# Three parts of an attention schedule moved: layer norm statistics six steps sooner, expert weights four steps later, the last output tile in the fourth step

## The chip, the cores and the metric

The kernel runs on one core of a Trainium2 chip. A core has a matrix engine (TensorE, written PE; PEld is its loading of weights), a vector engine (VectorE, DVE), an engine for activations (ScalarE, ACT), a general engine (GpSimd, POOL), and SyncE (SP), which here only issues transfers (DMAs). Each engine works through its own queue of instructions in order and waits on semaphores for the others. Matrix products land in PSUM banks; ACT or DVE must copy them out (evict them) before the bank is used again. The metric is the device time of one execution in microseconds, the median of several.

## The reference

For each of 16 batch elements of 512 tokens with 128 features, in float32:

```python
mod = (silu(c) @ wmod).reshape(16, 6, 1, 128)      # sa, ca, ga, sb, cb, gb
ga, gb = [(2*(g >= 0) - 1) * maximum(abs(g), 0.25) for g in (ga, gb)]
h = layernorm(x) * (1 + ca) + sa
x = x + ga * attention(h)            # 16 heads of 64, causal softmax, W_out, b_out
h = layernorm(x) * (1 + cb) + sb
logits = h @ Wr + br                 # 8 experts, the two largest are kept
weights = softmax(where(logits >= second_largest, logits, -inf))
expert_out = gelu(h @ W1 + b1) @ W2 + b2           # each expert, hidden size 512
x = x + gb * sum_over_experts(expert_out * weights)
```

## The kernel before

The kernel has two phases. The first does attention, both layer norms and the routing of tokens to experts; the second runs the experts over tiles of 256 routed rows and adds the results up. The change is in the first.

**Elements, pairs, steps.** The loop over `pairs` (near the end of the main function) goes over the 16 elements b and, in each, over 8 pairs of heads n = 0 to 7. One turn is a step; step n of element b is called step n below, counted from 0. `attend` writes out a step in a fixed order on PE, DVE, ACT and SP, because `manual_schedule` keeps the written order of these four engines; GpSimd's instructions are chained to their order by `Pinned`. In a step, PE does the scores of this pair (L446), z of the previous pair (L534), the q and k projection of the next pair (L410), then what `units` holds, then the transposes of the probabilities (L506). DVE takes the masked maxima (L463) and the reciprocals (L486), then what `c` holds, then copies two of the three transposed groups out of PSUM (L516). ACT takes the exponentials (L479), evicts z (L543) and q and k (L418), and copies the third transposed group (L516). POOL multiplies the probabilities by the reciprocals (L116, the helper line of all its pinned calls).

**PSUM.** The pool `ring` has four buffers of two banks, given out in turn. A product that takes a buffer waits until what stood in it four allocations earlier has been evicted.

**Work beside.** `BESIDE` says for each step which tasks of other elements go into it. `quiet` is behind this step's maxima on GpSimd, `a` and `b` stand between reciprocals on DVE, `units` on PE, `c` before the pT copies on DVE, `last` at the end. A letter names the element: `s` the next one (its first layer norm, transposition and v projection), `f` the previous one (output projection, second layer norm, router logits), `r` the one before that (routing), `m` this one. `BESIDE_LAST` holds the same for the last element. `1` is one indirect store of routed rows on GpSimd, two of them in steps 0 and 1.

The tasks that matter here:

- `ln0`, `ln1` (`layernorm`, L326 to L329): bn_stats and bn_aggr for two token tiles each, on DVE, and after the second an addition of epsilon. `dev` raises this to the power -0.5 on POOL; `norm0`, `norm1` (L338) normalise on DVE; `hT` transposes on PE and is evicted by ACT (L696). They serve the first norm (`s`) or the second (`f`).
- `o0`, `o1` (`project_out`): the output projection of token tiles 0 and 1, and 2 and 3: for each tile 8 head pairs with two column halves, 64 matmul instructions in the profile. `add0`, `add1` (`projected`, L615) add the bias on DVE; `x0`, `x1` (`attended`) multiply by the gate and add to x on POOL.
- `share`, `choose`, `count`, `rank`, `extend`, `place`, `pick`, `carry`: routing, small operations on DVE and one product on PE. `extend` starts at L828 with `lack`, `place` ends at L861; `pick` ends with the weights of the chosen experts (L873, L874).
- `load_x` (L137): the load of an element's x, issued by SP at step 0 of the element before it.

**SP at the start.** After the weights, SP issues in element 0 `load_rest` and, at the end of step 1, `lay_out` (L258 to L277): copies of the experts' weights within device memory and fills of the buffers `hs` (10 MB) and `ys` (1 MB) with zeros. Behind these come the loads of `mods` (L227, at the end of step 7) and of x_2 (at step 0 of element 1); x_0 and x_1 are loaded before all of it.

Of the kernel before, what the change touches and what calls it, by code (L numbers as in the profile page):

```python
# [9 lines left out]
FP = mybir.dt.float32  # L10
# [5 lines left out]
P = 128  # L16
# [5 lines left out]
def kernel(  # L22
# [65 lines left out]
    def bank(name):  # L88
        return banks(name)[:, 0, :]
# [43 lines left out]
    x_tiles = {}  # L133

    def load_x(b):
        x = work.tile([P, NT, D], FP, tag="x", name=f"x_{b}", bufs=3)
        nc.sync.dma_start(out=x, in_=resid[b].rearrange("(t p) d -> p t d", p=P))  # L137
        x_tiles[b] = x

# [383 lines left out]
    def z(b, n, ps=None):  # L523
        v, pT = v_tiles[b, n // (NP // VH)], pT_tiles.pop((b, n))
        col = n % (NP // VH) * P
        if ps is None:
            ps = bank(f"ps_z_{b}_{n}")


        for t in reversed(range(NT)):  # L530
            for own in (True, False)[: NT - t]:
                cols = slice(t * P, (t + 1) * P) if own else slice((t + 1) * P, S)
                for j in range(2):
                    nc.tensor.matmul(  # L534
                        ps[j * DH : (j + 1) * DH, cols],
                        v[:, t, col + j * DH : col + (j + 1) * DH],
                        pT[:, t, j, cols],
                        start=(t == NT - 1),
                        stop=(t == 0 and not own),
                    )  # L540
        zT = work.tile([P, S], FP, tag="zT", name=f"zT_{b}_{n}", bufs=NP + 2)
        zT_tiles[b, n] = zT
        return lambda: nc.scalar.copy(zT, ps)  # L543

# [50 lines left out]
    hT2 = {}  # L595
    attn_out = {}

    def project_out(b, half_of):
        ps = bank(f"ps_o_{b}_{half_of}")
        attn_out[b, half_of] = ps  # L600
        for t in range(2 * half_of, 2 * half_of + 2):
            for n in range(NP):
                in_columns(
                    ps[:, ts(t % 2, D)],
                    zT_tiles[b, n][:, ts(t, P)],
                    wo_sb[:, n, :],
                    start=(n == 0),
                    stop=(n == NP - 1),
                )

    def projected(b, half_of):
        if half_of == 0:
            attn_sum[b] = work.tile([P, NT, D], FP, tag="o", name=f"o_{b}", bufs=1)
        ps = attn_out.pop((b, half_of))
        nc.vector.tensor_tensor(  # L615
            attn_sum[b][:, 2 * half_of : 2 * half_of + 2, :],
            ps[:, : 2 * D].rearrange("p (t d) -> p t d", d=D),
            bo_sb.unsqueeze(1).to_broadcast([P, 2, D]),
            ALU.add,
        )  # L620

# [101 lines left out]
    def finishing(b):  # L723

        return in_parts(
            b,
            mods=(load_mods,),
            o0=(project_out, 0),
            o1=(project_out, 1),
            add0=(projected, 0),  # L730
            add1=(projected, 1),
            x0=(attended, 0),
            x1=(attended, 1),
            ln0=(layernorm, 1, 0),
            ln1=(layernorm, 1, 1),
            dev=(deviation, 1),
            off=(offset,),
            norm=(second_norm,),
            store=(store,),
            hT=(second_hT,),  # L740
            lg=(logits,),
            wt=(weights,),
            share=(share,),
        )
# [30 lines left out]
    def route(b):  # L775
# [85 lines left out]
            nc.vector.tensor_tensor(pos, pos, room, ALU.add)  # L861

        def pick():
            wt, _ = chosen_by.pop(b)
            chosen = tiles["chosen"]
            part = tmp("part", both)
            pos = tiles["pos"]
            nc.vector.tensor_tensor(part, chosen, pos.unsqueeze(1).to_broadcast(both), ALU.mult)
            where = tmp("where", [P, 2, NT])
            nc.vector.tensor_reduce(where, part, AX.X, ALU.add)  # L870
            slots_of[b] = tmp("slot", [P, 2, NT], I32, bufs=2)
            nc.vector.tensor_copy(slots_of[b], where)
            nc.vector.tensor_tensor(part, chosen, wt.unsqueeze(1).to_broadcast(both), ALU.mult)  # L873
            nc.vector.tensor_reduce(weight[:, :, at], part, AX.X, ALU.add)  # L874

# [8 lines left out]
        def experts():  # L884
# [21 lines left out]
            nc.sync.dma_start(out=rows_of[first], in_=in_dram.rearrange("s o -> o s"))  # L906

        parts = dict(
            choose=choose, count=count, rank=rank, extend=extend, place=place, pick=pick, carry=carry_on
        )  # L910
        if b in (LATE - 1, LAST):
            parts["experts"] = experts
# [200 lines left out]
    x2 = {}  # L1113

    def fetch_x(b):
        x2[b] = work.tile([P, NT, D], FP, tag="zT", name=f"x2_{b}", bufs=NP + 2)
        nc.sync.dma_start(out=x2[b], in_=kept(x_rows[b]))
        load_gate_b(b)

    def combine(b, width=NT):  # L1120

        x, got = x2.pop(b), got_tiles.pop(b)
        gb = gates_b.pop(b)
        y = work.tile([P, NT, D], FP, tag="zT", name=f"y_{b}", bufs=NP + 2)
        results[b] = y
        for t in range(0, NT, width):
            part = slice(t, t + width)
            for u in range(t, t + width):
                i = b * NT + u
                nc.scalar.activation(y[:, u, :], got[:, 0, u, :], AF.Identity, scale=weight[:, 0, i : i + 1])  # L1130
            for u in range(t, t + width):
                i = b * NT + u
                nc.vector.scalar_tensor_tensor(
                    y[:, u, :], got[:, 1, u, :], weight[:, 1, i : i + 1], y[:, u, :], ALU.mult, ALU.add
                )
            nc.vector.tensor_tensor(
                y[:, part], y[:, part], gb.unsqueeze(1).to_broadcast([P, width, D]), ALU.mult
            )
            nc.vector.tensor_tensor(y[:, part], y[:, part], x[:, part], ALU.add)
            if width < NT:  # L1140
                stored.setdefault(b, []).append(
                    nc.sync.dma_start(out=in_rows(out[b])[:, part], in_=y[:, part]).ins
                )
# [79 lines left out]
    def dense_rest(b):  # L1223

        h = work.tile([P, NT, D], FP, tag="hT1", name=f"rest_h_{b}")
        nc.sync.dma_start(out=h, in_=kept(h2_rows[b]))
        x = work.tile([P, NT, D], FP, tag="x", name=f"rest_x_{b}", bufs=3)
        load = nc.sync.dma_start(out=x, in_=in_rows(out[b]))
        behind_all(load.ins, stored.get(b, ()), "the element's output so far")
        hT = work.tile([P, S], FP, tag="hT2", name=f"rest_hT_{b}", bufs=1)  # L1230
# [26 lines left out]
    for task in later:  # L1257
# [2 lines left out]


    BESIDE = {
        0: dict(a="r.share", b="r.choose", quiet="1", units="f.o0 r.count", c="1 s.ln0 f.add0 r.rank",
                last="f.x0"),
        1: dict(quiet="1", units="f.o1", c="1 s.ln1 r.extend r.place f.add1", last="s.dev f.x1"),
        2: dict(b="s.norm0", quiet="1", units="v0", c="s.norm1 r.pick", last="rows"),
        3: dict(units="s.hT", c="f.ln0"),
        4: dict(quiet="1", units="v1", c="f.ln1 r.carry", last="f.dev"),
        5: dict(a="f.off", quiet="1", units="s.v0", c="f.norm"),
        6: dict(quiet="1", units="s.v1 f.hT", last="f.store"),  # L1270
        7: dict(units="f.lg", c="f.wt", last="m.mods"),
    }

    BESIDE_LAST = {
        0: dict(a="r.share", b="r.choose", quiet="1", units="f.o0 r.count", c="1 f.add0 r.rank", last="f.x0"),
        1: dict(quiet="1", units="f.o1", c="1 r.extend r.place f.add1", last="f.x1"),
        2: dict(quiet="1", units="v0", c="r.pick", last="rows"),
        3: dict(quiet="1", units="v1", c="1 f.ln0 r.carry", last="r.experts"),
        4: dict(quiet="1", c="1 f.ln1", last="f.dev"),
        5: dict(a="f.off", quiet="1", c="1 f.norm"),  # L1280
        6: dict(quiet="1", units="f.hT", c="1", last="f.store"),
        7: dict(units="f.lg o01234", c="f.wt", late="o56", last="m.mods"),
    }

    FIRST = {
        0: dict(units=[begin["v0"], begin["v1"], modulation_matmuls], c=[modulation_rows], last=[load_rest]),
        1: dict(units=[transposed_b1], c=[copied_b1], last=[lay_out]),
    }
    ends = finishing(LAST)
    for at, (b, n) in enumerate(pairs):  # L1290
        prev = pairs[at - 1] if at else None
        nxt = pairs[at + 1] if at + 1 < len(pairs) else None
        if n == 0 and b + 1 < B and b + 1 not in x_tiles:
            load_x(b + 1)
        if n == 7 and b < LAST:
            routes[b - 1] = route(b - 1) if b else {}
        known = {
            "s": starting(b + 1) if b + 1 < B else {},
            "f": finishing(b - 1) if b else {},
            "r": routes.get(b - 2, {}) | ({"share": finishing(b - 2)["share"]} if b > 1 else {}),  # L1300
            "m": finishing(b),
# [57 lines left out]
        10: ["share"],  # L1359
    }  # L1360
    steps = {at: [ends[name] for name in names] for at, names in steps.items()}
    for at, name in enumerate(("share", "choose", "count", "rank", "extend", "place", "pick", "carry")):
        steps.setdefault(1 + at, []).append(routes[LATE][name])
    for k, part in enumerate([*routes[LAST].values(), left_here, left_all]):
        steps.setdefault(11 + k, []).append(part)
# [93 lines left out]
```

## Time and profile before

| what | value |
|---|---|
| median of 3 executions | 1553.93 us (1552.44 to 1553.98) |
| the profiled execution's own time | 1554.75 us |
| its span, first to last instruction | 1552.9 us |
| PE / DVE / ACT / POOL busy | 97% / 71% / 68% / 62% |
| granted TensorE clock, mean | 0.993 |
| one element of the first phase (element 8, eight steps) | 77.8 us |

The table and the numbers of the prediction come from one profiled execution. The page gives busy times over the whole span; the windows give them for a stretch (sum, mean, clock and the transfers' share at the end of a line); the timeline lists instructions with start, duration, engine, line, operation, output and inputs, and in square brackets how long the engine stood idle before it and what ended that wait. A step is measured here from the first scores matmul to the first scores matmul of the next step. Busy time of PE is modelled at its ends, so a full PE in a window says that it had work, not that it ran at its peak.

### The profile page before, as it was taken

The page shows a single profiled execution, that of the slowest core. Times are in us where ns is not written, and L with a number is a line of the kernel's source. Part 1 is how long each engine was busy: PE and PEld are TensorE (multiplying, and loading weights), DVE is VectorE, ACT ScalarE, POOL GpSimd, SP SyncE. Part 2 cuts the span into 40 slices and gives each one's busy share as a digit, 9 for nine tenths or more (in the row PEclk, how much of TensorE's full clock was granted, in tenths as well). Part 3 has the DMA queues.
Part 4 walks back from the last instruction along what each step waited for, and adds up shares of the span by engine and source line. Part 5 has one row for each costly group of instructions (what it writes and reads, how often), then busy time and mean ns, then how long its engine had stood idle before and what let it go on. Part 6 is the DMA issues. An engine that isn't in the chain of part 4 may idle for free. (4 is left out here: it accounts for less than half of the span.)

```text
span 1552.9 us, 45385 instructions
## 1 busy us (share of the span) xinstructions
PE 1506.9 (97%) x16760; PEld 1042.5 (67%) x16760; DVE 1098.2 (71%) x4264; ACT 1062.5 (68%) x2885; POOL 964.1 (62%) x1555
## 2 busy tenths in 40 slices
PE   6999999999999999999999999999999999999994
PEld 3565656565656565656666666666666679999994
DVE  4767787878787878787878787878787844443434
ACT  4767777777777777777777777777777754444543
POOL 3445556666666666666666666666666656667653
PEclk9999999999999999999999999999999999999997
DMA  3860101010101010101010101010100047799994
GB/s 112 216 185 9 36 12 36 22 36 22 36 22 36 22 36 22 36 22 36 22 36 22 36 23 36 22 36 22 36 22 29 28 139 246 239 348 317 308 305 141
DMA packets 97902, 130.79 MB, mean 84 GB/s; under 512 B 10777, under 2 KB 73166, under 8 KB 97674
## 3 DMA queue, kind: packets, MB, share of 16 engines
q1 hardware_dynamic: 86777, 102.17, 21.4%
q0 software_dynamic: 10608, 24.73, 4.6%
q8 instruction: 135, 2.21, 0.6%
q10 hardware_dynamic: 288, 0.92, 0.2%
q14 instruction: 94, 0.76, 0.2%
HBM read 86.95 MB, written 46.07 MB: 86 GB/s over the span
## 5 line engine op out<-in xcount | busy, mean ns | idle before, releaser
L479 ACT ACTIVATE p<-p,nmax 128x512 f32<-128x512 f32 (+3 forms) x1024 | 560.3, 549 | 216.6 <-DVE nmax L463 216.6
L116 POOL TENSOR_SCALAR p<-p,rden 128x512 f32<-128x512 f32 (+3 forms) x1024 | 527.9, 533 | 240.4 <-DVE rden L486 233.4
L463 DVE CUSTOM_DVE_ANT_0 p<-sc,mask 128x512 f32<-128x512 f32 (+3 forms) x1024 | 439.9, 485 | 12.8 <-PE sc L446 12.4
L516 DVE COPY pT<-ps_pT 128x1024 f32<-128x1024 f32 (+2 forms) x384 | 276.5, 771 | 82.5 <-PE ps_pT L506 81.9
L446 PE MATMUL sc<-qk 64*128 64x512 f32 (+3 forms) x2048 | 312.8, 443 | 4.2 <-DVE pT L516 1.5
L534 PE MATMUL ps_z<-pT,v 128*64 128x128 f32 x3556 | 303.5, 322 | 0.2
L116 POOL DMA_INDIRECT hs<-rows,slot x128 | 134.8, 1053 | 215.4 <-DVE nmax L463 143.7
L446 PEld LDWEIGHTS sc<-qk 64*128 64x128 f32 x2048 | 185.5, 189 | 117.6 <-DVE pT L516 57.5
L534 PEld LDWEIGHTS ps_z<-pT,v 128*64 128x64 f32 x3556 | 200.5, 137 | 33.8 <-PE sc L446 0.5
L506 PEld LDWEIGHTS ps_pT<-ident,p 64*128 64x128 f32 x5120 | 177.2, 139 | 64.2 <-POOL p L116 56.8
L506 PE MATMUL ps_pT<-ident,p 64*128 64x64 f32 x5120 | 201.6, 226 | 10.3 <-POOL p L116 6.9
L1019 ACT ACTIVATE hid<-ps_h,wexp 128x256 f32<-128x256 f32 x272 | 106.8, 476 | 128.0 <-issue 120.0
L479 ACT ACTIVATION_READ_ACCUMULATOR p<-p,nmax 128x1 f32 x1024 | 191.3, 187 | 0.0
L486 DVE RECIPROCAL rden<-den 128x2 f32<-128x2 f32 x512 | 84.0, 164 | 146.3 <-ACT p L479 141.8
L116 POOL DMA_INDIRECT ys<-yrow,to_rows x136 | 134.9, 992 | 63.6 <-issue 28.0
L516 ACT COPY pT<-ps_pT 128x768 f32<-128x768 f32 x128 | 102.1, 798 | 98.7 <-PE ps_pT L506 96.1
L410 PE MATMUL ps_qk<-hT,wq_sb 128*64 128x512 f32 x512 | 132.6, 596 | 0.9 <-ACT hT L696 0.9
L410 PE MATMUL ps_qk<-hT,wk_sb 128*64 128x512 f32 x512 | 132.5, 596 | 0.0
L1032 PE MATMUL ps_e<-wexp,hid 128*128 128x128 f32 x1088 | 132.4, 275 | 0.0
L418 ACT COPY qk<-ps_qk 128x1024 f32<-128x1024 f32 x128 | 128.6, 1005 | 3.8 <-PE ps_qk L410 3.8
L1017 PE MATMUL ps_h<-hsT,wexp 128*128 128x256 f32 x544 | 129.5, 381 | 1.3 <-DVE hsT L1005 1.3
L1032 PEld LDWEIGHTS ps_e<-wexp,hid 128*128 128x128 f32 x1088 | 126.8, 192 | 0.1
(140 smaller groups left out, 1490.2 us busy)
## 6 DMA issues: line engine op xcount, KB each, us to landing
wexp<-wall SPq DMA_DIRECT2D x68, 578.0 KB
hs<-empty SPq DMA_DIRECT2D x1, 10062.0 KB
hrow<-hs SPq DMA_DIRECT2D x68, 129.0 KB
rows<-h_rows SPq DMA_DIRECT2D x32, 256.0 KB
got<-ys POOLq DMA_DIRECT2D x15, 512.0 KB, 5.2
x<-in_L_attn_resid_dram SPq DMA_DIRECT2D x16, 256.0 KB
mods<-mods_rows SPq DMA_DIRECT2D x16, 256.0 KB
x_rows<-x SPq DMA_DIRECT2D x16, 256.0 KB
```

Source lines behind the costliest of these rows:

```text
L116: made = getattr(nc.gpsimd, name)(*args, **kw)
L410: nc.tensor.matmul(out[r], lhsT[:, r], rhs, **flags)
L418: evictions.append(lambda: nc.scalar.copy(qk, ps))
L446: nc.tensor.matmul(ps[:, j, off : off + w], qk[r, 0, ts(i, P)], qk[r, 1, :w], start=True, stop=True)
L463: masked = nc.vector.tensor_tensor_reduce(out=p[:, j, r], in0=ps[:, j, r], in1=mask[:, S - (i + 1) * P : S], scale=-QSCALE, scalar=-MASKED ...
L479: nc.scalar.activation(p[:, j, r], p[:, j, r], AF.Exp, bias=nmax[:, j : j + 1], scale=-1.0, accum_out=den[:, j : j + 1])
L506: nc.tensor.transpose(ps[:, h, off + 2 * t + j, :], p[rows, j, at + t * P : at + (t + 1) * P], ident[rows, rows],)
L516: engine_copy(pT[:, : 2 * (i + 1), ts(i, P)].rearrange("p k (h q) -> p k h q", h=2), ps[:, :, off : off + 2 * (i + 1), :].rearrange("p h k ...
L534: nc.tensor.matmul(ps[j * DH : (j + 1) * DH, cols], v[:, t, col + j * DH : col + (j + 1) * DH], pT[:, t, j, cols], start=(t == NT - 1), st ...
L1017: nc.tensor.matmul(parts[j], wts[:, ts(j, P)], hT, start=True, stop=True)
L1019: nc.scalar.activation(hid[:, j, :], parts[j], AF.Gelu, bias=wts[:, ROWW - NHC + j : ROWW - NHC + j + 1])
L1032: nc.tensor.matmul(ps[:, ts(c, D)], hid[:, j, ts(c, P)], wts[:, HID + j * D : HID + (j + 1) * D], start=(j == 0), stop=(j == NHC - 1),)
```

## The change

Three tasks move, and two pools grow to allow it.

- The first layer norm's `ln0`, `ln1` and `dev` leave steps 0 and 1, where they served the next element (`s`), for steps 5 and 6, where they serve the element after the next (`t`, two ahead). x is therefore loaded at step 4, two elements ahead, and the pool of x has 4 buffers. Element 1's statistics, which no earlier element can take, stand in `FIRST`, in steps 0 and 1 of element 0, where they were.
- The output projection is cut into three parts, token tiles 0 and 1, tile 2, and tile 3: `o1` and `add1` in step 1 are half as large, and `o2`, `add2` and `x1` stand in step 3. In step 1, `add1` stands ahead of `extend` and `place`; in step 3, `add2` ahead of `ln0`. The zT pool has one more buffer, since tile 3 of all eight pairs is read until step 3.
- The weights of the chosen experts become a task of their own, `weigh`, in step 6; `pick` keeps the slots in step 2.
- For the last element, `v1` moves from step 3 to step 4, and `o2` takes its place.

```diff
     def load_x(b):
-        x = work.tile([P, NT, D], FP, tag="x", name=f"x_{b}", bufs=3)
+        x = work.tile([P, NT, D], FP, tag="x", name=f"x_{b}", bufs=4)
...
-        zT = work.tile([P, S], FP, tag="zT", name=f"zT_{b}_{n}", bufs=NP + 2)
+        zT = work.tile([P, S], FP, tag="zT", name=f"zT_{b}_{n}", bufs=NP + 3)
...
+    OUT = ((0, 1), (2,), (3,))
+
+    def project_out(b, part):
+        ps = bank(f"ps_o_{b}_{part}")
+        attn_out[b, part] = ps
+        for k, t in enumerate(OUT[part]):
             for n in range(NP):
                 in_columns(
-                    ps[:, ts(t % 2, D)],
+                    ps[:, ts(k, D)],
...
-    def projected(b, half_of):
-        if half_of == 0:
+    def projected(b, part):
+        if part == 0:
             attn_sum[b] = work.tile([P, NT, D], FP, tag="o", name=f"o_{b}", bufs=1)
-        ps = attn_out.pop((b, half_of))
+        ps = attn_out.pop((b, part))
+        n = len(OUT[part])
         nc.vector.tensor_tensor(
-            attn_sum[b][:, 2 * half_of : 2 * half_of + 2, :],
-            ps[:, : 2 * D].rearrange("p (t d) -> p t d", d=D),
-            bo_sb.unsqueeze(1).to_broadcast([P, 2, D]),
+            attn_sum[b][:, OUT[part][0] : OUT[part][0] + n, :],
+            ps[:, : n * D].rearrange("p (t d) -> p t d", d=D),
+            bo_sb.unsqueeze(1).to_broadcast([P, n, D]),
             ALU.add,
         )
...
+        def weigh():
+            wt, _ = chosen_by.pop(b)
+            chosen = tiles["chosen"]
+            part = tmp("part", both)
             nc.vector.tensor_tensor(part, chosen, wt.unsqueeze(1).to_broadcast(both), ALU.mult)
             nc.vector.tensor_reduce(weight[:, :, at], part, AX.X, ALU.add)
...
     BESIDE = {
-        0: dict(a="r.share", b="r.choose", quiet="1", units="f.o0 r.count", c="1 s.ln0 f.add0 r.rank",
-                last="f.x0"),
-        1: dict(quiet="1", units="f.o1", c="1 s.ln1 r.extend r.place f.add1", last="s.dev f.x1"),
+        0: dict(a="r.share", b="r.choose", quiet="1", units="f.o0 r.count", c="1 f.add0 r.rank", last="f.x0"),
+        1: dict(quiet="1", units="f.o1", c="1 f.add1 r.extend r.place"),
         2: dict(b="s.norm0", quiet="1", units="v0", c="s.norm1 r.pick", last="rows"),
-        3: dict(units="s.hT", c="f.ln0"),
+        3: dict(units="s.hT f.o2", c="f.add2 f.ln0", last="f.x1"),
         4: dict(quiet="1", units="v1", c="f.ln1 r.carry", last="f.dev"),
-        5: dict(a="f.off", quiet="1", units="s.v0", c="f.norm"),
-        6: dict(quiet="1", units="s.v1 f.hT", last="f.store"),
+        5: dict(a="f.off", quiet="1", units="s.v0", c="f.norm t.ln0"),
+        6: dict(quiet="1", units="s.v1 f.hT", c="r.weigh t.ln1", last="f.store t.dev"),
         7: dict(units="f.lg", c="f.wt", last="m.mods"),
     }
 
     BESIDE_LAST = {
-        0: dict(a="r.share", b="r.choose", quiet="1", units="f.o0 r.count", c="1 f.add0 r.rank", last="f.x0"),
-        1: dict(quiet="1", units="f.o1", c="1 r.extend r.place f.add1", last="f.x1"),
+        0: BESIDE[0],
+        1: BESIDE[1],
         2: dict(quiet="1", units="v0", c="r.pick", last="rows"),
-        3: dict(quiet="1", units="v1", c="1 f.ln0 r.carry", last="r.experts"),
-        4: dict(quiet="1", c="1 f.ln1", last="f.dev"),
+        3: dict(quiet="1", units="f.o2", c="1 f.add2 f.ln0 r.carry", last="f.x1 r.experts"),
+        4: dict(quiet="1", units="v1", c="1 f.ln1", last="f.dev"),
         5: dict(a="f.off", quiet="1", c="1 f.norm"),
-        6: dict(quiet="1", units="f.hT", c="1", last="f.store"),
+        6: dict(quiet="1", units="f.hT", c="1 r.weigh", last="f.store"),
...
+    second = starting(1)
     FIRST = {
-        0: dict(units=[begin["v0"], begin["v1"], modulation_matmuls], c=[modulation_rows], last=[load_rest]),
-        1: dict(units=[transposed_b1], c=[copied_b1], last=[lay_out]),
+        0: dict(
+            units=[begin["v0"], begin["v1"], modulation_matmuls],
+            c=[modulation_rows, second["ln0"]],
+            last=[load_rest],
+        ),
+        1: dict(units=[transposed_b1], c=[copied_b1, second["ln1"]], last=[lay_out, second["dev"]]),
     }
...
-        if n == 0 and b + 1 < B and b + 1 not in x_tiles:
-            load_x(b + 1)
+        if n == 4 and b + 2 < B:
+            load_x(b + 2)
...
             "s": starting(b + 1) if b + 1 < B else {},
+            "t": starting(b + 2) if b + 2 < B else {},
```

## The prediction

> **What bounds the kernel now.** I read the page first, then the windows of one element's eight steps, then the timeline of VectorE (DVE) in two of them, then SyncE's (SP's) timeline of the first 110 us.
>
> ```profile
> PE 1506.9 (97%) x16760; PEld 1042.5 (67%) x16760; DVE 1098.2 (71%) x4264; ACT 1062.5 (68%) x2885; POOL 964.1 (62%) x1555
> ```
>
> TensorE (PE) is busy 97%, so only its idle time can be won, or new idle time added. Element 8 by steps (start:end, length, PE, PEld, DVE, ACT, POOL):
>
> ```profile
> 652.03:663.16 11.13, 11.13 (x162) 8.39 (x160) 9.13 (x40) 6.76 (x20) 8.52 (x13) 1.00 0.05 14
> 663.16:672.52 9.36, 9.36 (x108) 5.40 (x104) 8.31 (x33) 7.66 (x21) 6.18 (x11) 1.00 0.20 65
> 672.52:681.73 9.21, 8.72 (x107) 5.25 (x103) 7.64 (x28) 7.26 (x21) 4.19 (x9) 1.00 0.01 3
> 681.73:691.14 9.41, 9.41 (x103) 5.49 (x102) 7.45 (x32) 7.61 (x21) 6.00 (x10) 1.00 0.03 9
> ```
>
> These are the element's steps 1 to 4; all eight are 77.85 us. The chain of work gives PE's fixed part: scores 2.21, z 2.32, q and k 1.72, transposes 1.39, together 7.64; a half of v is 1.72, 64 matmuls of the output 3.49. Steps 1 and 2 are just that sum (11.13, 9.36). Step 3 has 7.64 and about 0.37 of hT transposes, 8.01, and takes 9.21: 1.20 idle, the only room of size for more PE work.
>
> Step 1 on DVE, from the timeline:
>
> ```profile
> 658.78 0.17 DVE L486 RECIPROCAL rden<-den 128x2 f32<-128x2 f32 x1 [0.60 <-ACT p L479]
> ...
> 659.87 0.17 DVE L828 TENSOR_TENSOR lack<-upto,rooms 128x8 f32<-128x8 f32 x1
> ...
> 661.74 0.22 DVE L861 TENSOR_TENSOR upto<-upto,room 128x32 f32<-128x32 f32 x1
> ...
> 661.98 0.42 DVE L615 TENSOR_TENSOR o<-ps_o,bo_sb 128x256 f32<-128x256 f32 x1
> ...
> 662.62 1.82 DVE L516 COPY pT<-ps_pT 128x1024 f32<-128x1024 f32 x2 [0.22 <-PE ps_pT L506]
> ...
> 663.90 0.19 PEld L446 LDWEIGHTS sc<-qk 64*128 64x128 f32 x2 [0.49 <-DVE pT L516]
> ```
>
> DVE is free at 658.95, and copies from 662.62; the last row shows PE's next scores waiting for that copy. So the pT copy's start, called C below, is where DVE reaches PE: work on DVE is hidden only until C. In a step bound by PE, C comes 0.53 before the step's end (10.59 of 11.13). In step 2 it comes 0.33 late (9.15 of 9.35) and the scores after it end 0.26 late: PE goes on as if its step began at C + 0.46. In step 5 there is room:
>
> ```profile
> 699.95 1.23 DVE L516 COPY pT<-ps_pT 128x1024 f32<-128x1024 f32 x1 [1.89 <-PE ps_pT L506]
> ```
>
> Last, SP's queue at the start, and what DVE waited for:
>
> ```profile
> 60.92 33.62 SPq L277 DMA_DIRECT2D ys<-empty  x1
> 94.59 7.24 SPq L227 DMA_DIRECT2D mods<-mods_rows  x1
> 101.87 0.43 SPq L137 DMA_DIRECT2D x<-in_L_attn_resid_dram  x1
> ```
>
> ```profile
> 75.43 1.82 DVE L516 COPY pT<-ps_pT 128x1024 f32<-128x1024 f32 x2 [1.89 <-PE ps_pT L506]
> ```
>
> ```profile
> 106.40 0.29 DVE L326 BATCH_NORM_STATS2 st<-x 128x6 f32<-128x128 f32 x1 [6.04 <-DMA x<-in_L_attn_resid_dram]
> ```
>
> The load of x_2 sits behind the 10 MB zero fill and goes out at 101.87; DVE, wanting it at 100.36, waited to 106.40.
>
> **1. The statistics six steps sooner: element 0.** t.ln0 for x_2 now stands in element 0's step 5. The load moves up on SP too, but still behind the fill: in SP's order it takes the place of mods_0, whose issue began at 94.59. DVE reaches the statistics at 73.5 (last rden 73.37 + 0.17) and stops. Queued behind them on DVE are the pT copies; behind these PE's scores, so ACT and POOL too. When it lands: in that slot mods_0's DMA packets ran from 102.0 to 104.8, and x_2's last packet (105.84) came 0.56 before DVE went on. So 104.8 + 0.56 = 105.4; bounds 102.6 (first packet) and 106.4 (as now). Then two bn_stats/bn_aggr pairs, 0.81 to the copy as in step 3 (679.74 to 680.54): C = 106.2 where it was 75.43, **+30.8**.
>
> After some 29 us without work PE may be slow. At the start of this run the same groups show it:
>
> ```profile
> 11.79 1.97 PE L410 MATMUL ps_qk<-hT,wq_sb 128*64 128x512 f32 x4 [0.87 <-ACT hT L696]
> ...
> 20.55 1.08 PE L410 MATMUL ps_qk<-hT,wq_sb 128*64 128x512 f32 x4
> ```
>
> The excess over full speed until then, by group: hT 0.68, q 0.94, k 0.89, scores 1.66, 4.2 in all, with PE idle in between. So 0 to 4.2; I take half, **+2.1**, since PE will come back denser. The granted clock reads 1.00 in both stretches, so the durations carry this, not that row.
>
> The Trainium skill ("TensorE: Matmul & The Clock Gate", Part 1) says that an idle window of about 3.4 us halves the clock, until about 3.4 us of sustained work. That would make 1.7 instead of 2.1 and the total 0.4 less. The row above ran at half speed far longer than 3.4 us, so it differs on the length; no row shows PE after such a wait in mid run.
>
> **2. Element 1.** x_2 is no longer awaited in its step 0 (11.87 to 11.13: 7.64 + 3.49), and step 1 (13.10) has no routing yet: 7.64 + 1.745 = 9.385. In step 3 C moves to 9.61 by part 4's rows, PE goes on from 10.07, and with step 4's 9.35 that is 19.42 against 8.89 + 9.41 now: 1.1 lost. -0.74 - 3.72 + 1.1 = **-3.3**.
>
> **3. Step 1 of elements 2 to 14.** PE sheds 32 matmuls, 1.745. The two bn pairs and the rstd add (658.87 to 659.87, 1.0) leave DVE. But add1 now stands ahead of extend and place and must wait for its matmuls. Measured from the step's start: before, PE's 64 ended at 9.90, so 32 end at 8.155; add1, 128 columns, 0.30 (between 0.17 for a tiny operation and 0.42 for 256; the ends change the term by 0.13) ends at 8.50. The train from lack to L861 is 2.09, overlapping by 0.08 at both ends: C = 10.43, against 10.59 (662.62 - 652.03) now. The freed 1.745 becomes waiting for DVE; 0.16 is won.
>
> Step 2 loses the two weight operations (L873, L874), 0.47. Now from first masked max to C is 7.62, then 7.15, and the next masked max follows C by 2.07. C falls to 19.71 (DVE 10.43 + 2.07 + 7.15 = 19.65; PE 10.43 + 0.46 + 8.82 = 19.71) against 20.28: 0.57 ahead. Step 3 begins at 20.24 (now 20.49).
>
> **4. Step 3 and 4.** o2 comes after hT: done at 20.24 + 8.155 + 0.37 = 28.77. add2 runs 28.82 to 29.12, then ln0, 0.81: C = 29.85. PE alone would allow 20.24 + 9.77 - 0.53 = 29.48. Today C is 28.52, but the next scores wait for hT's eviction on ACT (ends at 29.65), so masked max starts at 30.99; then it starts at 29.85 + 2.07 = 31.92. Step 4's DVE work is 7.34 to C (PE would reach it at 39.13): 39.26 against 38.57. **Net +0.65 per element**, 13 elements: **+8.45**. Bounds: PE's sum alone (-1.745 in step 1, 9.77 - 9.21 = +0.56 in step 3, -0.05 in step 4), -1.24; the delay of C in step 3 not absorbed at all, +1.33. I take +0.65, since each wait is a measured row.
>
> **5. Element 15.** In step 3 o2 replaces v1, and add2 and ln0 stand ahead of carry: C moves from 8.81 to 8.42 + 1.97 (ln0 start to C now) = 10.39. **+1.6** if nothing after it absorbs the delay; bounds +0.1 (PE's sum: step 4 with v1 9.36 against 9.22) and +2.3 (the three operations of experts, 0.75 on DVE in step 4, on top).
>
> **6. What costs nothing.** t.ln0 in step 5 (0.8) fits the 1.89 above; t.ln1 and weigh in step 6 (1.0 + 0.47) fit its 2.08 idle; without that cover they cost 0.8 and 1.5. POOL: dev (1.05) runs after step 6's divides, before step 7's, which find POOL idle 4.9; x1 (two of 0.73) ends about 10.4 after step 3's start, before step 4's scatter at 12.6. SP: the loads of later x go out behind the rows loads (done at 669.5 in element 8) and are wanted at 698; x_rows waits for the later x1 with nothing urgent behind. The fourth x and eleventh zT buffer only take room. In the expert phase two small operations become a part of their own beside a PE that is full.
>
> **Sum.** 30.8 + 2.1 - 3.3 + 8.45 + 1.6 = +39.65 on the profiled execution's own 1554.75 (span 1552.9) is 1594.4. That execution is 0.8 above the median 1553.93, so **1593.6**. 0.2%, 3.1 us, is about what a measurement of this kernel tells from no change.
>
> **Rivals.**
> - **PE's sum holds** (adds and copies have more slack than I see): -1.24 x 13 = -16.1 for +8.45, element 1 -3.6, element 15 +0.1: +13.3, 1567. For: PE is 97% busy. Against: the scores' wait for the copy.
> - **DVE's waits add up**: +1.33 x 13 = 17.3 for 8.45, 1602. For: three PE-bound steps follow and recover nothing. Against: ACT already holds step 3.
> - **Not slower: x_2 lands before 73.5**, its load not held by the fill. The 32.9 goes, and the per-element bounds leave 1534 to 1561, middle 1548. It is not slower if the element term is under +0.13; with DVE waiting, a landing after about 92 outweighs even PE's sum. Against: ys alone held SP until 94.5.
>
> **How the numbers follow.** Forecast 0.72; PE's sum 0.10; waits add up 0.11; early load 0.03; other costs unseen 0.04. The forecast's own range, by the landing (-2.8, +1.0), the slow PE (2.1 each way) and the element term (0.3 each way, 4), is 1584 to 1601. 1577 to 1603 leaves out most of the PE-sum case and the early load, and half of the upper one. Faster 0.03 and same 0.01 come from the early load and the PE-sum tail; the rest is slower.
>
> **What would show it.** A DVE wait of about 32 us on x's load at L326 near 73.5; PE idle near 77 to 107 and its next groups up to twice their length; in step 1 the add standing 1.2 idle for ps_o ahead of the routing and C 10.4 after the first scores, so that step 2's scores, begun at 9.4, stretch from 2.38 to near 3.9; in step 3 C at 9.6; step 5 unchanged at 9.36. The forecast is wrong if no such wait stands at L326, or if step 1's C comes near 8.9.

## The result, and the profile after

| | before | after |
|---|---|---|
| median of 4 executions each | 1553.18 us (1551.42 to 1553.98) | 1593.88 us (1592.67 to 1594.88) |
| ratio, with its 95% interval | 1 | 1.0269 (1.0256 to 1.0282) |
| the profiled execution: own time, span | 1554.75, 1552.9 | 1594.88, 1593.0 |
| granted TensorE clock, mean | 0.993 | 0.985 |

The changed kernel is 2.7% slower: 40.7 us between the medians, 40.1 between the two profiled spans. The forecast was 1593.6. Two terms of its sum were off by several microseconds and cancelled, so the total says less than the parts; those follow.

First the page of the changed kernel: busy time by engine, the slices of PE and of its clock, shares of the chain that ended last, and the scores' group (busy and mean ns, then idle time before it and what ended that).

```profile
PE 1517.3 (95%) x16760; PEld 1043.8 (66%) x16760; DVE 1106.7 (69%) x4279; ACT 1059.8 (67%) x2885; POOL 962.0 (60%) x1555
PE   6939999999999999999999999999999999999994
PEclk9969999999999999999999999999999999999997
PE 70%; DVE 10%; ACT 9%; POOL 4%; issue 3%; SPq 2%; DMA 1%; DVEq 0%; POOLq 0%; ACTq 0%
L446 PE MATMUL sc<-qk 64*128 64x512 f32 (+3 forms) x2048 | 323.1, 448 | 39.4 <-DVE pT L516 36.6
```

PE has the same 16,760 matmuls and went from 97% to 95%. The hole is in the third slice, about 80 to 119 us, and the scores wait 36.6 us in all for DVE's pT copy.

Why, is in SP's and DVE's timelines of that stretch (start, duration, engine, line, operation, output and inputs):

```profile
60.96 31.30 SPq L277 DMA_DIRECT2D ys<-empty  x1
92.32 7.22 SPq L137 DMA_DIRECT2D x<-in_L_attn_resid_dram  x1
```

```profile
73.19 0.17 DVE L486 RECIPROCAL rden<-den 128x2 f32<-128x2 f32 x1 [0.60 <-ACT p L479]
103.29 0.29 DVE L326 BATCH_NORM_STATS2 st<-x 128x6 f32<-128x128 f32 x1 [29.94 <-DMA x<-in_L_attn_resid_dram]
...
104.11 2.12 DVE L516 COPY pT<-ps_pT 128x1024 f32<-128x1024 f32 x3
```

DVE reaches the statistics of x_2 at about 73.3, in step 5 of element 0, and stands for 29.94 us, because SP issued the load of x_2 only after the zero fill, at 92.32. The pT copy behind the statistics starts at 104.11; before it was at 75.43. The windows (start:end, length, then PE, PEld, DVE, ACT, POOL, granted clock, share and rate of the transfers) and PE's timeline show the rest:

```profile
76.00:105.00 29.00, 1.51 (x8) 0.41 (x6) 1.64 (x5) 0.47 (x1) 0.00 (x0) 0.59 1.01 275
105.00:110.00 5.00, 4.64 (x38) 3.73 (x40) 4.80 (x21) 3.13 (x11) 1.24 (x2) 0.66 0.00 0
110.00:114.70 4.70, 4.70 (x59) 2.15 (x56) 1.79 (x8) 3.95 (x11) 3.82 (x8) 1.00 0.00 0
```

```profile
105.36 1.65 PE L446 MATMUL sc<-qk 64*128 64x256 f32 x8 [27.85 <-DVE pT L516]
106.94 3.10 PE L534 MATMUL ps_z<-pT,v 128*64 128x128 f32 x28
109.87 1.03 PE L410 MATMUL ps_qk<-hT,wq_sb 128*64 128x512 f32 x4
```

PE, DVE, ACT and POOL stop for about 28 us (PE for 27.85). Afterwards z takes 3.10 where its usual 28 matmuls take 2.39, and the next q group is at its usual 1.03: PE came back slow, which cost 0.7 to 1.0 us. Here the granted clock shows it: a window from 81.2 to 105.3 reads 0.50, one from 105.36 to 108.4 also 0.50, and one from 108.45 to 110 reads 1.00. So PE ran at half clock for about 3.1 us after its return.

Split by the elements of the first phase, after minus before, in us: element 0 **+29.46**, element 1 **-3.20**, elements 2 to 14 together **+12.76**, element 15 **+1.48**, the rest (the last step and the experts) -0.28, and -0.1 from the first instruction to element 0's first scores. The first phase goes from 1256.0 to 1296.4.

A typical element shows where the 12.76 comes from (median length of each step, elements 2 to 14):

| step | 0 | 1 | 2 | 3 | 4 | 5 | 6 | 7 | sum |
|---|---|---|---|---|---|---|---|---|---|
| before | 11.34 | 11.13 | 9.35 | 9.23 | 9.41 | 9.35 | 9.73 | 8.31 | 77.85 |
| after | 11.34 | 9.38 | 10.53 | 10.02 | 9.63 | 9.52 | 9.73 | 8.74 | 78.89 |

Steps 1 to 4 of element 8, to be laid against the four rows shown for before:

```profile
683.91:693.30 9.39, 9.39 (x132) 6.65 (x128) 6.56 (x29) 6.76 (x20) 6.81 (x11) 1.00 0.03 10
693.30:703.82 10.52, 9.85 (x107) 5.67 (x103) 9.39 (x37) 7.49 (x21) 5.21 (x10) 1.00 0.19 57
703.82:713.84 10.02, 10.02 (x132) 6.87 (x134) 6.79 (x29) 7.27 (x21) 4.81 (x9) 1.00 0.04 10
713.84:723.48 9.64, 9.63 (x108) 5.35 (x104) 8.09 (x33) 7.67 (x21) 6.47 (x12) 1.00 0.10 36
```

Step 1 has shed its 32 matmuls and is 1.74 shorter; step 2 has the same work on PE and is 1.16 longer, and step 3 has 0.81 more. Step 1 hands on what it saved as a wait. DVE's timeline at the end of this step 1, and the weight load of the next scores:

```profile
690.67 0.17 DVE L486 RECIPROCAL rden<-den 128x2 f32<-128x2 f32 x1 [0.60 <-ACT p L479]
692.12 0.29 DVE L618 TENSOR_TENSOR o<-ps_o,bo_sb 128x128 f32<-128x128 f32 x1 [1.28 <-PE ps_o L410]
692.32 0.18 DVE L833 TENSOR_TENSOR lack<-upto,rooms 128x8 f32<-128x8 f32 x1
...
694.10 0.22 DVE L866 TENSOR_TENSOR upto<-upto,room 128x32 f32<-128x32 f32 x1
694.23 2.14 DVE L516 COPY pT<-ps_pT 128x1024 f32<-128x1024 f32 x3
```

```profile
695.50 0.73 PEld L446 LDWEIGHTS sc<-qk 64*128 64x128 f32 x8 [1.10 <-DVE pT L516]
```

The add waits 1.28 for its matmuls, the routing train stands behind the add, the copy behind the train: C is 10.32 after the step's first scores, and the step ends on PE at 9.39. In step 3 the add waits again:

```profile
712.66 0.29 DVE L618 TENSOR_TENSOR o<-ps_o,bo_sb 128x128 f32<-128x128 f32 x1 [1.76 <-PE ps_o L410]
...
713.68 1.19 DVE L516 COPY pT<-ps_pT 128x1024 f32<-128x1024 f32 x1
```

The prediction did not have the next one. Step 6 of element 6 (it begins at 575.22), DVE, then POOL:

```profile
582.04 0.17 DVE L486 RECIPROCAL rden<-den 128x2 f32<-128x2 f32 x1 [0.60 <-ACT p L479]
582.12 1.46 DVE L882 TENSOR_TENSOR part<-chosen,wt 128x64 f32<-128x64 f32 x1
...
584.75 1.82 DVE L516 COPY pT<-ps_pT 128x1024 f32<-128x1024 f32 x2
```

```profile
580.02 4.13 POOL L116 TENSOR_SCALAR p<-p,rden 128x512 f32<-128x512 f32 x8
```

The first operation of `weigh` lasts 1.46 beside POOL's multiplications of p by the reciprocals (L116), called the divides here. In the kernel before the same operation is L873, in step 2 and after the divides. Its tile row there (min, median and max in ns):

```profile
L873 DVE TENSOR_TENSOR part<-chosen,wt x16: 213/219/221, 204.8 to 1340.0; 128x64 f32<-128x64 f32 x16
```

With it and `ln1` DVE's work in step 6 outgrows its idle time, C comes 9.53 into the step, and the lateness is in step 7: 8.74 for 8.31.

### The profile page after: what moved, and what is told of

Read it like the earlier page. It is cut to its first block, busy times and chain, and to the rows that moved or that the text cites. A ratio compares the mean times of both kernels' runs of the same rounds, so it can differ in the third digit from the quotient of the medians.

```text
span 1593.0 us, 45407 instructions
## 1 busy us (share of the span) xinstructions
PE 1517.3 (95%) x16760; PEld 1043.8 (66%) x16760; DVE 1106.7 (69%) x4279; ACT 1059.8 (67%) x2885; POOL 962.0 (60%) x1555
## 4 chain that ended last, share of the span: by engine, by line
PE 70%; DVE 10%; ACT 9%; POOL 4%; issue 3%; SPq 2%; DMA 1%; DVEq 0%; POOLq 0%; ACTq 0%
PE sc L446 14%; PE ps_z L534 12%; PE ps_qk L410 9%; PE ps_e L1048 8%; PE ps_h L1033 7%; ACT p L479 7%; PE ps_pT L506 7%; PE ps_o L410 7%; DVE pT L516 4%; PE ps_v L410 4%; POOL p L116 3%; DVE p L463 2%; SPq L277 2%; DMA x<-in_L_attn_resid_dram 1%; DVE part L882 1%
## 5 line engine op out<-in xcount | busy, mean ns | idle before, releaser
L116 POOL TENSOR_SCALAR p<-p,rden 128x512 f32<-128x512 f32 (+3 forms) x1024 | 526.2, 530 | 251.2 <-DVE rden L486 236.8
L446 PE MATMUL sc<-qk 64*128 64x512 f32 (+3 forms) x2048 | 323.1, 448 | 39.4 <-DVE pT L516 36.6
L116 POOL DMA_INDIRECT hs<-rows,slot x128 | 134.3, 1050 | 231.7 <-DVE nmax L463 171.8
L506 PE MATMUL ps_pT<-ident,p 64*128 64x64 f32 x5120 | 196.5, 226 | 4.0 <-POOL p L116 2.4
L116 POOL DMA_INDIRECT ys<-yrow,to_rows x136 | 135.3, 995 | 60.0 <-issue 29.7
```

Of the source, the lines that this page charges most:

```text
L116: made = getattr(nc.gpsimd, name)(*args, **kw)
L446: nc.tensor.matmul(ps[:, j, off : off + w], qk[r, 0, ts(i, P)], qk[r, 1, :w], start=True, stop=True)
L506: nc.tensor.transpose(ps[:, h, off + 2 * t + j, :], p[rows, j, at + t * P : at + (t + 1) * P], ident[rows, rows],)
```

## The experiments

Theory: three causes add up. (1) x_2 is loaded behind the fill, and everything waits for it once. (2) `add1` and `add2` wait for their matmuls with DVE's later work behind them. (3) `weigh` in step 6 is long beside POOL's divides, and with `ln1` it overruns. Rivals: without the wait in element 0 another takes its place or the clock drops anyway; the output split, not its order on DVE, is at fault; the long operation in step 6 is long by itself or waits for data.

The experiments ran four to a chip. On these chips the kernel before took 1570.12 (first four) and 1566.55 us (last four). The expert phase took 307 to 321 us in their traces against 297 in the two profiles above; the first phase of the changed kernel repeated within 0.5 us (1296.4 and, in e8_changed, 1296.9). So each time is compared through its ratio to the kernel before on its own chip, and each cause through the first phase (1256.0 before, 1296.4 after). The kernel before left no trace on these chips.

**e1_early: x_2 ahead of the fill.**

```diff
 FIRST, step 0:
-            last=[load_rest],
+            last=[load_rest, lambda: load_x(2)],
 ...
-        if n == 4 and b + 2 < B:
+        if n == 4 and 2 < b + 2 < B:
```

> The changed kernel with one thing different: x_2 is loaded at the end of element 0's first step, ahead of the zero fill. Theory (the wait for x_2 behind the fill is 29.5 of the 40.7 us lost, and nothing else stands behind it): element 0 back to 77.1 us, no DVE wait at L326, no drop of the granted clock, about 1564.4 us, so still slower than before by about 11. Rival (the wait only covers another late transfer, mods_0 or x_3, which stay behind the fill): a new wait in element 1 and a time between 1570 and 1590.

Measured: 1588.77 us, ratio 1.0117 (1.0096 to 1.0138); first phase 1267.5. The same window as above:

```profile
76.00:105.00 29.00, 28.93 (x352) 19.04 (x352) 19.78 (x76) 20.84 (x58) 14.74 (x27) 1.00 0.86 242
```

SP's timeline of this kernel shows the load where it now goes out:

```profile
31.30 0.43 SPq L137 DMA_DIRECT2D x<-in_L_attn_resid_dram  x1
```

PE is full and at full clock, L326 waits for x only once in the whole run, 0.7 us at its very start, and no new wait has come: element 1 takes 76.84 as in the changed kernel (76.82). Against the changed kernel in its own run here (e8_changed, 1296.9) the first phase is 29.4 shorter. That is a net figure: element 0 is 31.3 shorter, of which 1.6 is a quicker start of this execution (see the last section), and elements 2 to 14 are 2.1 longer together, which is not explained. So cause 1 is shown, with its size to about 2 us, and so is what is left without it: 11.5 us in the first phase. The ratio says 18.6 us in all; the other 7 lie in the expert phase, which was the longest of all in this execution (320.7), and are not explained.

**e2_swap: e1, with the order of DVE's work turned round.**

```diff
-        1: dict(quiet="1", units="f.o1", c="1 f.add1 r.extend r.place"),
+        1: dict(quiet="1", units="f.o1", c="1 r.extend r.place f.add1"),
-        3: dict(units="s.hT f.o2", c="f.add2 f.ln0", last="f.x1"),
+        3: dict(units="s.hT f.o2", c="f.ln0 f.add2", last="f.x1"),
 last element:
-        3: dict(quiet="1", units="f.o2", c="1 f.add2 f.ln0 r.carry", last="f.x1 r.experts"),
+        3: dict(quiet="1", units="f.o2", c="1 f.ln0 r.carry f.add2", last="f.x1 r.experts"),
```

> The early load, and the order on DVE turned round: in step 1 extend and place ahead of add1, in step 3 ln0 ahead of add2 (last element likewise). Theory (the freed PE time of step 1 is lost because DVE waits with its routing train behind the add, which waits for PE): the pT copy in step 1 comes 9.1 after the first scores where it came 10.3, step 3 becomes PE's sum of 9.8, steps 1 to 5 of an element fall by about 1.7 us against the changed kernel; about 1541 us, faster than before. Rival (DVE has too much work in these steps whatever its order, or PE's moved half is the cost): as the early load alone, about 1564.

Measured: 1571.65, ratio 1.0013 (0.9995 to 1.0031); first phase 1253.0, 14.5 less than e1 and 3.0 less than before, a quarter of the gain expected. The mean of elements 2 to 14 is 77.9 for e1's 79.0, so the order is worth 1.1 us an element: cause 2 is shown. The rest went into two places. Step 7 is still 8.74. And step 1 fell short; its DVE timeline (the step begins at 492.69):

```profile
499.69 0.26 DVE L833 TENSOR_TENSOR lack<-upto,rooms 128x8 f32<-128x8 f32 x1
499.99 0.43 DVE L836 TENSOR_TENSOR need<-lack,tile_rows 128x16 f32<-128x16 f32 x1
...
502.16 0.28 DVE L618 TENSOR_TENSOR o<-ps_o,bo_sb 128x128 f32<-128x128 f32 x1
502.36 1.81 DVE L516 COPY pT<-ps_pT 128x1024 f32<-128x1024 f32 x2
```

Started 1.0 us sooner after the last reciprocal than in the kernel before, the train meets more of POOL's divides, which end at 501.08, and its first operations stretch: `lack` 0.26 for 0.17, `need` 0.43 for 0.24, and the scan behind them (L844) 0.45 for 0.24. The train lasts 2.55 where 2.09 was reckoned with; C is 9.67 instead of 9.1.

**e3_weigh: e1, with `ln1` moved from step 6 to step 5.**

```diff
-        5: dict(a="f.off", quiet="1", units="s.v0", c="f.norm t.ln0"),
-        6: dict(quiet="1", units="s.v1 f.hT", c="r.weigh t.ln1", last="f.store t.dev"),
+        5: dict(a="f.off", quiet="1", units="s.v0", c="f.norm t.ln0 t.ln1"),
+        6: dict(quiet="1", units="s.v1 f.hT", c="r.weigh", last="f.store t.dev"),
```

> The early load, and ln1 moved from step 6 to step 5 (behind ln0), so that weigh stands alone in step 6. Theory (the first weight operation lasts 1.46 us instead of 0.22 beside POOL's divides, and with ln1's 1.05 that overruns the 2.08 that DVE has in step 6, which costs step 7 its 0.42): the operation still lasts about 1.46, but step 7 is 8.31 again and step 5 stays within 0.1 of 9.52; about 13 x 0.42 = 5.5 less than the early load alone, 1559 us. Rival (step 7 is late for another reason, for instance dev on POOL): 1564, step 7 still at 8.74.

Measured: 1578.95, ratio 1.0049 (1.0032 to 1.0065); first phase 1263.9. Step 7 is back at 8.31, and the mean element 0.45 shorter than e1's; over 13 elements that is 5.9, of which element 0, 2.1 longer than in e1 from a slower start of this execution, hides a part. The long operation itself has not changed:

```profile
L882 DVE TENSOR_TENSOR part<-chosen,wt x16: 215/1458/1467, 238.2 to 1356.8; 128x64 f32<-128x64 f32 x16
```

So the 0.43 in step 7 is the overrun of two tasks together in step 6; alone, even the long `weigh` is hidden.

**e6_weigh_last: e1, with `ln1` ahead of `weigh` in step 6.**

```diff
-        6: dict(quiet="1", units="s.v1 f.hT", c="r.weigh t.ln1", last="f.store t.dev"),
+        6: dict(quiet="1", units="s.v1 f.hT", c="t.ln1 r.weigh", last="f.store t.dev"),
```

> The early load, and in step 6 weigh behind ln1 instead of ahead of it. Theory (the first weight operation waits for a gap in POOL's divides, which end about 8.9 after the first scores): begun near 7.9 it lasts at most 1.1 and ends with the divides, about 9.1; step 7 falls from 8.74 to about 8.5. Rival (it takes 1.46 wherever it stands in this step, POOL or not): it ends at 9.4 and step 7 stays at 8.74.

Measured: 1570.18 (one execution, no interval); first phase 1261.1, 6.5 less than e1's; step 7 at 8.31 in the median, where 8.5 was expected. DVE and POOL in step 6 of an element (it begins at 542.83):

```profile
550.65 0.49 DVE L329 TENSOR_SCALAR rstd<-mv 128x4 f32<-128x4 f32 x1
551.04 0.39 DVE L882 TENSOR_TENSOR part<-chosen,wt 128x64 f32<-128x64 f32 x1
...
551.89 1.22 DVE L516 COPY pT<-ps_pT 128x1024 f32<-128x1024 f32 x1 [0.20 <-PE ps_pT L506]
```

```profile
547.63 4.08 POOL L116 TENSOR_SCALAR p<-p,rden 128x512 f32<-128x512 f32 x8
```

The same instruction on the same data, in the same step, takes 0.39 when it starts 0.67 before the divides end (551.71), and 1.46 when it starts 2.03 before. The expectation had allowed it up to 1.1. It is not long by itself. Nor does it wait for data: `wt` is complete since step 0, and DVE works through its queue in order in both. Its length goes with the divides still ahead on POOL. Cause 3 is shown as to place and size. Operations with one input are not all spared: L329 takes 0.49 here, and in the kernel before it took 0.17 in element 8's step 1 and 0.51 in its step 4, beside the divides there (689.25).

What it waits for is not shown, but a rule bears on it. The Trainium skill, "SBUF — State Buffer", section "SBUF: two separate sides", says that VectorE and GpSimd share a pair of ports as an exclusive lock, which an instruction holds to its end, and that a VectorE operation takes part in it when it has two SBUF inputs (against a GpSimd operation that reads SBUF) or runs in a two-port performance mode. L882 has two such inputs, and bn_stats, with one, stayed at 0.28 beside the same divides. For these two the kind agrees; whether L329 runs in a two-port mode no run shows. The size does not, if the lock is handed over at the holder's end: the divides of that step last 0.36 to 0.69 each, so one of them would make at most 0.22 + 0.69 = 0.91 (an estimate from these rows), and 1.46 was measured: three divides ended while L882 stood.

**e4_out: the kernel before, with the output split alone.** The three parts of the output as in the changed kernel, `add1` left last in step 1, the statistics and weights where they were.

```diff
-        1: dict(quiet="1", units="f.o1", c="1 s.ln1 r.extend r.place f.add1", last="s.dev f.x1"),
+        1: dict(quiet="1", units="f.o1", c="1 s.ln1 r.extend r.place f.add1", last="s.dev"),
...
-        3: dict(units="s.hT", c="f.ln0"),
+        3: dict(units="s.hT f.o2", c="f.add2 f.ln0", last="f.x1"),
...
```

> The kernel before with the output's cut alone: o1 and add1 half as large in step 1, o2, add2 and x1 in step 3 (in the last element as in the changed kernel); statistics, weights and the load of x stay where they were. Theory (step 1 is bound by DVE as soon as PE sheds work, and add2 ahead of ln0 delays step 3): about +0.6 us for each of 13 elements and +1.5 in the last, about 1562 us. Rival (the move balances PE and only the statistics and weights cost): PE's sum, 1.24 less for each element, about 1537 us.

Measured: 1583.93, ratio 1.0084 (1.0067 to 1.0101); first phase 1266.5. Medians of steps 1 to 3: 10.45, 9.68, 10.23 where 11.13, 9.35, 9.23 were. Step 1 (it begins at 497.43) on DVE:

```profile
504.30 0.17 DVE L486 RECIPROCAL rden<-den 128x2 f32<-128x2 f32 x1 [0.60 <-ACT p L479]
...
505.40 0.39 DVE L833 TENSOR_TENSOR lack<-upto,rooms 128x8 f32<-128x8 f32 x1
...
507.57 0.29 DVE L618 TENSOR_TENSOR o<-ps_o,bo_sb 128x128 f32<-128x128 f32 x1
507.76 1.22 DVE L516 COPY pT<-ps_pT 128x1024 f32<-128x1024 f32 x1
```

C is 10.33 with no wait for the add at all: the statistics (the gap between the first two rows), the train and the add are DVE's own work, and fill the step past PE's 9.39. By itself the split loses 0.87 us an element (0.6 expected): it takes 1.74 of PE's work out of a step that DVE then bounds, and puts it into step 3, where it costs 1.00 in spite of the 1.20 idle that PE had there. `add2` stands ahead of `ln0` in this run too, so what the 1.00 owes to that order is not separated from what it owes to the moved matmuls.

**e7_stats: the kernel before, with the statistics' move alone**, x_2 loaded early, four x buffers.

```diff
-        0: dict(a="r.share", b="r.choose", quiet="1", units="f.o0 r.count", c="1 s.ln0 f.add0 r.rank",
+        0: dict(a="r.share", b="r.choose", quiet="1", units="f.o0 r.count", c="1 f.add0 r.rank",
-        1: dict(quiet="1", units="f.o1", c="1 s.ln1 r.extend r.place f.add1", last="s.dev f.x1"),
+        1: dict(quiet="1", units="f.o1", c="1 r.extend r.place f.add1", last="f.x1"),
...
-        5: dict(a="f.off", quiet="1", units="s.v0", c="f.norm"),
-        6: dict(quiet="1", units="s.v1 f.hT", last="f.store"),
+        5: dict(a="f.off", quiet="1", units="s.v0", c="f.norm t.ln0"),
+        6: dict(quiet="1", units="s.v1 f.hT", c="t.ln1", last="f.store t.dev"),
...
```

> The kernel before with the statistics' move alone (ln0, ln1 and dev in steps 5 and 6 two elements ahead) and x_2 loaded ahead of the zero fill. Theory (steps 0 and 1 are PE's sums there, so work taken off DVE buys nothing, and step 5 and 6 have room for it): every step of elements 2 to 14 as in the kernel before within 0.05 us; element 1 about 2.2 us shorter; ratio about 0.9985. Rival (DVE helps to set steps 0 and 1): steps 0 or 1 shorter by 0.2 or more, 0.99.

Measured: 1567.52, ratio 0.9994 (0.9980 to 1.0009); first phase 1251.7. The mean element is 77.82 for 77.84: DVE freed by 0.8 to 1.0 us in steps 0 and 1 changes nothing, since these steps are PE's sum. Two steps missed the 0.05 us that was expected, step 1 with 11.24 for 11.13 and step 3 with 9.10 for 9.23; they cancel. Of the 4.4 us by which the first phase is shorter, 2.76 are element 1, where x_2 was awaited before, and 1.6 a quicker start of that execution.

**e5_best: e1, e3's move and the mended order together**, with `extend` between the reciprocals, clear of the last stretch.

```diff
-        1: dict(quiet="1", units="f.o1", c="1 f.add1 r.extend r.place"),
+        1: dict(b="r.extend", quiet="1", units="f.o1", c="1 r.place f.add1"),
...
-        3: dict(units="s.hT f.o2", c="f.add2 f.ln0", last="f.x1"),
+        3: dict(units="s.hT f.o2", c="f.ln0 f.add2", last="f.x1"),
-        5: dict(a="f.off", quiet="1", units="s.v0", c="f.norm t.ln0"),
-        6: dict(quiet="1", units="s.v1 f.hT", c="r.weigh t.ln1", last="f.store t.dev"),
+        5: dict(a="f.off", quiet="1", units="s.v0", c="f.norm t.ln0 t.ln1"),
+        6: dict(quiet="1", units="s.v1 f.hT", c="r.weigh", last="f.store t.dev"),
 last element:
-        3: dict(quiet="1", units="f.o2", c="1 f.add2 f.ln0 r.carry", last="f.x1 r.experts"),
+        3: dict(quiet="1", units="f.o2", c="1 f.ln0 r.carry f.add2", last="f.x1 r.experts"),
```

> The changed kernel with the early load, ln0 ahead of add2 in step 3 (in the last element ln0 and carry), ln1 in step 5 so that weigh is alone in step 6, and in step 1 extend moved up between the two last reciprocals, with place and then add1 before the copy. Theory (the turned order gained only 3 us because the routing train, started sooner, ran beside POOL's divides and took 2.55 instead of 2.09; with extend in the gap of the reciprocals DVE reaches the copy before PE does): steps 1 to 4 become PE's sums, 9.4, 9.4, 9.9, 9.4, step 7 is 8.3; about 76.8 us for an element where the kernel before has 77.85, the first phase about 18 us shorter than before, ratio about 0.989. Rival (extend there delays the last reciprocal and with it POOL's divide and the transposes by as much): first phase within 4 us of the kernel before.

Measured: 1555.91, ratio **0.9921** (0.9902 to 0.9941): 0.8% below the kernel before, a small gain with an interval clear of 1. The first phase is 1243.2, 12.8 less than before (18 expected). Median steps 11.33, 9.48, 9.56, 9.99, 9.36, 9.45, 9.73, 8.31, in sum 77.2 where 77.85 was. DVE in step 1 (it begins at 490.08):

```profile
496.31 0.58 DVE L833 TENSOR_TENSOR lack<-upto,rooms 128x8 f32<-128x8 f32 x1
...
499.10 0.28 DVE L618 TENSOR_TENSOR o<-ps_o,bo_sb 128x128 f32<-128x128 f32 x1
499.30 1.21 DVE L516 COPY pT<-ps_pT 128x1024 f32<-128x1024 f32 x1
```

PE is back at 97%. C is 9.22, 0.36 later than the 8.86 at which PE would reach it (0.53 before the end of 9.39). DVE works without a pause from 496.22 to this copy, and `lack` and `need`, now in the midst of the divides, take 0.58 and 0.43 instead of 0.17 and 0.24, which is 0.60 more. Steps 1 and 2 come out 0.30 above PE's sums, 3.9 us over 13 elements, of the 5.2 that are missing; another 0.1 an element lies in step 5 (9.45 for 9.35), since step 4's copy comes 8.99 into that step.

**e8_changed: the changed kernel beside e5_best, e6_weigh_last and e7_stats.** No edit.

> The changed kernel itself on the chip of these runs, as the yardstick for the others: the first phase about 40 us longer than the kernel before, of it 29.5 in element 0, 1.0 in each of elements 2 to 14.

Measured: 1607.8, ratio 1.0267 (1.0243 to 1.0291), as in the first comparison (1.0269); first phase 1296.9, median steps equal to those of the first profile within 0.07.

## Why the prediction was right, and where not

The mechanisms of its parts 1 to 5 stood, and the forecast case happened; part 6 failed. That the total came out within 0.3 us is luck: -3.4 and +4.3 nearly cancel. By its parts:

- **1, the wait in element 0:** right in kind and place, too large by 3.4 of 32.9 (measured +29.46). Two terms were mis-sized. The landing was taken at 105.4, and DVE went on at 103.29, because the fill's last issue ended at 92.26 and not at 94.54; why it ended sooner is open. So C came at 104.11 instead of 106.2 (28.7 for 30.8). And slow PE cost 0.7 to 1.0 instead of 2.1: PE was slow for about 3.1 us, near the 3.4 us that the Trainium skill ("TensorE: Matmul & The Clock Gate", Part 1) gives, and far from the 10 us of the run's start, from which the term was taken. The clock row was also misread: it did show the slow stretch here (0.50), and the 1.00 at the run's start is a window for which the trace has no entry of the clock (see the last section).
- **2, element 1:** -3.20 for -3.3.
- **3, step 1:** the add's wait 1.28 (about 1.2), its end 8.50 into the step (8.50), C 10.32 (10.43). Step 2's scores stretched to 3.12, not near 3.9; C of step 2 at 19.54 (19.71), step 3's start at 19.91 (20.24). All a little sooner, by up to 0.33.
- **4, steps 3 and 4:** C at 29.77 (29.85), step 4's at 39.12 (39.26). By the start of step 6 the median steps give -1.75 + 1.18 + 0.79 + 0.22 + 0.17 = +0.61 an element; forecast +0.65. Step 5 was to stay as it was; its 0.17 is step 4's lateness handed on.
- **5, element 15:** +1.48 for +1.6.
- **6, what costs nothing: the step that failed.** `t.ln1` and `weigh` were put at 1.0 + 0.47 within 2.08 of idle time. The 0.47 came from rows of step 2, where POOL had finished; in step 6 the first of the two operations is 1.46 long instead of 0.22, the sum is 2.7, and step 7 grows by 0.43 in an element. Over 13 elements that is the miss of this term: 12.76 for 8.45, against 0.43 x 13 = 5.6, less the 0.04 an element by which parts 3 and 4 were too high, and less what elements 2 and 14 fell short of the others (they lost 0.40 and 0.61, not 1.04): 4.0 of the 4.3. e3_weigh and e6_weigh_last show it. The prediction priced an operation from a row in other company, and named idle time as the cover without asking what runs beside it. With it the element term, 12.76, left the 4 us either way that the prediction gave it, and lies midway between its 8.45 and the 17.3 of the rival "DVE's waits add up"; but the excess is in step 7, not in the waits that this rival names.

Of the rivals, "PE's sum holds" is what a cured kernel gets half way to: e5_best, without the early wait and with the order mended, takes 0.65 us off an element, of the 1.24 which that rival reckoned with. "Not slower, because x_2 lands before 73.5" needed its load ahead of the fill: e1_early makes just that, and is still slower, 1.0117, since the element term stays well above the +0.13 named as its limit. The prediction's 1534 to 1561 for that case was also too narrow by its own numbers: its upper end uses +0.65 an element, while the bound that it names, +1.33, gives 1569.

## What to carry to other kernels

When a task is moved to an earlier step, follow its loads through the issuing queue as well: here one load behind a 10 MB fill stopped four engines for about 28 us, and the same load issued 61 us sooner cost nothing. Work taken off the bounding engine is won only if the engine that follows it, here DVE with the pT copy behind everything else, is ready sooner as well; what must wait for late matmuls belongs last in front of that copy. Take the duration of a moved operation from a row with the same neighbour on the other engine, not only from the same shape.

## What the runs showed of the hardware that was not expected

- A DVE operation on two SBUF operands of 128x64 took 0.22 us alone, 0.39 near the end of POOL's divides and 1.46 in their midst; two small routing operations, of 128x8 and 128x16, 0.58 and 0.43 there for 0.17 and 0.24.
- After 28 us without work PE ran at a granted clock of 0.50 for about 3.1 us. At the start of the run its groups are up to twice their length for about 10 us. The windows print 1.00 there, but the table of the clock in the trace has no entry yet: in the kernel before the first one, of full clock, begins at 19.88, and the q group at 20.55 is the first near its usual length (1.08). The first step of element 0 took 9.93 us in the three executions where this entry begins at 14.6 to 16.2 (e1_early, e6_weigh_last, e7_stats), and 11.5 to 12.2 in the seven where it begins at 19.7 to 21.4. So this is what the text calls a quicker or slower start; a missing entry must not be read as full clock.
- The expert phase took 297 us in the two first profiles and 307 to 321 in the experiments' traces; for the changed kernel alone, 296.6 and 306.6, with the first phase alike. What sets this is open. In the experiments step 0's pT copy also starts at 10.9 to 11.0 into the step instead of 10.8, and step 1 is 0.1 longer where PE bounds it; why is open as well.
